# Two banded-mixing layers on one core: new instruction tables for both layers, three kinds of work moved between engines, and a setup in another order

## The chip, the cores and the metric

The kernel runs on one core of a Trainium2 chip. Its time is the device time of one launch in microseconds (us), of which the median over several runs counts; lower is better. The profile shows one execution. Its engines are called PE (TensorE, with PEld for its weight loads), DVE (VectorE), ACT (ScalarE), POOL (GpSimd) and SP (SyncE, which here only issues transfers). A name with q behind it (SPq, ACTq) is the engine's queue that issues transfers.

## The reference

The input `x` is a 512 x 512 image with 64 channels in float32. Two layers of the same form follow each other; each adds to `x` what it computes from a group norm of `x` over the whole image:

```python
def _gn(v, G=32, eps=1e-5):
    B_, H_, W_, C_ = v.shape
    g = v.reshape(B_, H_, W_, G, C_ // G)
    m = jnp.mean(g, axis=(1, 2, 4), keepdims=True)
    s = jnp.var(g, axis=(1, 2, 4), keepdims=True)
    return ((g - m) / jnp.sqrt(s + eps)).reshape(v.shape)
...
xn = _ln(x, norm_scale, norm_bias)
left = (xn @ Wl + bl) * mask * jax.nn.sigmoid(xn @ Wlg + blg)
right = (xn @ Wr + br) * mask * jax.nn.sigmoid(xn @ Wrg + brg)
out_gate = jax.nn.sigmoid(xn @ Wog + bog)
out = _banded_ingoing(left, right, WIN)
out = _ln(out, out_norm_scale, out_norm_bias) * out_gate
return out @ Wo + bo
```

There are 128 hidden channels. `_banded_ingoing` multiplies, per hidden channel, a band matrix of half width 4 (taken from `left` near the diagonal of the image) with `right`, so that each output row mixes the 9 nearest rows. The second layer cannot begin before the first has seen the whole image, since its group norm needs the sums over all of it.

## The kernel before

**Tiling.** The image's rows are cut into 9 blocks of 64 rows that overlap (`row_blocks`, line 145). In a block the columns are taken in two halves side by side on the 128 partitions and go through in 32 units of 8 columns, 8 units to a chunk, so a layer has 36 chunks and 288 units. A unit on its input side is loaded (`load`, line 474, two transfers into one of 12 z buffers), multiplied by the group norm's factor `ga` (`scaled`, line 515) and shifted by `gb` (`moved`, line 518), reduced to its layer norm's statistics (`inner_stats`, line 521), centred and rescaled, turned by TensorE (`transposed`, line 532), copied from PSUM twice (`kept`, `kept_again`), multiplied with the weights (`right`, line 587), gated, and written into the tile `RO`. On its output side, 16 units later, it passes the band product (`mix`, line 668), the second norm (`norm`, line 771), its gate, two more products, and is added to the image that `fetch` (line 819) has read anew and `stored` (line 852) writes.

**The bands.** Five extra units with negative numbers carry the pixels near the diagonal (`lefts`, `load_near`, line 485). They are loaded into the tile `A`, pass the same scaling, and give the band values `L9`, which `spread_left` writes to a table in HBM (`left_of`). From there `take_left` (line 654) reads one slab of the band matrices for the current block into `A`, four transfers of 128 KB a slab and eight slabs a block. The table is first filled with zeros from the tile `nothing`.

**The order.** All instructions of the layers go through `en` (line 458), which keeps them in program order on their engine. That order is written out by hand in two tables of 320 words, `FIRST` and `SECOND` (lines 38 and 71), one for each layer. `layer` (line 868) runs through its table once for each period, a period being one chunk of eight units. A word such as `norm6:0!@2` names a step, its part, how many units it lies behind the period's first (so `load:11` loads unit 11 while unit 0 is the period's own), with `!` for the step's other engine, and the PSUM buffer behind `@`. For `norm` the mark means POOL in place of ACT, for `copy` (the band product's way out of PSUM) DVE in place of ACT. `on_load` (line 909) also takes one waiting slab, ahead of the unit's own load. `on_copy` puts a slab in the list once the last chunk of a block has used it. Every transfer of the layers is issued by SP.

**The setup.** `fetch_layer` (line 264) issues some 70 small loads of weights and masks on ACT's queue. `input_stats` (line 397) streams the whole image through three buffers `gn_x`, 16 transfers of 4 MB on SP, and takes `bn_stats` on DVE; between the tiles `solve_layer` (line 297) folds the weights. Then the sums are closed on DVE and TensorE, `ga` and `gb` come out (`group_affine`, line 390), and the first layer begins. Between the layers `mid_stats` (line 1074) does the same from sums that the first layer has collected.

Of the kernel before, what the change touches and what calls it, by code (L numbers as in the profile page):

```python
# [43 lines left out]
last:0 fetch:1 end:0 turn0:1@1 move:11 copy:7 turn1:1@1 proj0:0@0 right1:0 tg:1 norm3:2 sig0:0
resc:2 resc:1 norm4:2 band:0@2 ost1:4 norm1:2 copy:0 right0:0 norm5:2! gate:2@1 ztr:1@0 scale:8
gated:2 norm6:2! sums:-2 last:1 keep0:1 keep1:1 fetch:2 ost0:7 ost2:5 norm2:2! stp:0 inner:6
norm7:2! band:1@2 sums:0 ztr:2@0 copy:1 ost0:5 keep0:2 turn1:2@1 ost1:6 inner:11 norm0:2! load:12
turn0:2@0 inner:5 proj0:1@2 move:8 keep1:2 sa:4 inner:8 norm0:3 scale:12 centre:9 tg:2 sig0:1
band:4@0 sd0:4 norm1:3 end:1 norm3:3! band:6@1 load:13 norm6:3 norm2:3! norm7:3! right0:1 sd1:4
resc:3 copy:4 sd2:4 gate:3@2 stp:-3 norm5:3! copy:6 gated:3 fetch:3 norm4:3! proj0:2@0 turn1:3@1  # L50
centre:4 turn0:3@2 band:5@2 tg:3 sig0:2 centre:6 norm2:4 right0:2 last:2 ztr:3@1 copy:5 end:2
gate:4@2 ost2:9 keep0:3 proj1:1@0 norm6:4! ost2:11 norm5:4! norm0:4 gated:4 load:14 norm7:4
norm3:4! ost2:12 norm1:4! sig1:1 last:3 scale:13 norm4:4 scale:14 sums:-1 ost2:15 ost1:13
turn1:4@2 centre:5 keep1:3 ost3:8 ost3:11 turn0:4@2 gate:5@1 resc:4 gated:5 ost2:10 ost0:11 resc:6
ost1:11 right1:1 tg:4 proj1:2@0 norm5:5! norm7:5! norm4:5! proj0:3@2 ost2:8 ost1:10 norm6:5
ztr:4@1 norm2:5! sig1:2 sig0:3 norm1:5! end:3 centre:8 keep0:4 right1:2 resc:5 right0:3 sums:3
fetch:4 norm3:5 norm0:5 keep1:4 last:4 centre:7 ost3:12 turn1:5@2 load:15 ost0:10 turn0:5@1 end:4
norm6:6 norm7:6! norm1:6 proj1:3@0 centre:10 tg:5 sig1:3 proj0:4@1 sig0:4 stp:-1 proj1:4@2 ost3:10
right1:3 norm4:6! ost1:8 ztr:5@0 norm5:6! sig1:4 fetch:5 right0:4 norm0:6 sums:1 ost0:8 keep0:5
ost3:9 last:5 sums:2 right1:4 load:16 gate:6@1 resc:7 keep1:5 ost1:9 ost0:9 gate:7@2 ost3:14 sa:8  # L60
ost3:13 turn0:6@0 norm2:6! norm3:6! gated:6 gated:7 norm0:7 ost0:14 sd0:8 scale:15 stp:1 fetch:7
move:15 turn1:6@0 sd1:8 norm4:7! norm1:7! centre:11 tg:6 fetch:6 end:5 proj1:5@1 proj0:5@2 sig1:5
ztr:6@0 norm7:7! norm5:7! norm6:7 load:17 sig0:5 norm2:7 right1:5 sums:4 keep0:6 last:6 norm3:7!
move:13 right0:5 ztr:7@2 keep1:6 keep0:7 keep1:7 turn0:7@0 turn1:7@1 sd2:8 proj0:6@1 proj1:6@2
tg:7 stp:3 stp:2 end:6 scale:17 norm5:8! resc:8 load:18 norm4:8 sig0:6 stp:4 fetch:8 sig1:6
# [3 lines left out]
seed:0 inner:8 turn1:1@2 inner:5 ztr:1@0 right1:0 move:11 ost3:5 stp:-1 keep0:1 turn0:1@2 norm5:2!  # L69
last:0 keep1:1 norm0:2 tg:1 inner:10 norm2:2 resc:2 centre:4 norm6:2! proj0:1@1 sa:4 sig0:1  # L70
proj1:1@0 norm7:2 end:0 sig1:1 right0:1 band:4@2 copy:4 ztr:2@1 right1:1 band:5@0 centre:5
centre:6 keep0:2 keep1:2 stp:0 sd0:4 norm3:2 seed:1 gate:2@2 inner:11 copy:5! fetch:2 norm4:2
norm1:2! gated:2 centre:3 proj0:2@1 turn0:2@0 turn1:2@2 band:7@2 norm0:3! norm7:3 sd1:4 last:1
resc:3 norm2:3! sig0:2 tg:2 norm3:3! gate:3@0 norm6:3 sd2:4 copy:7 norm4:3! norm5:3 norm1:3
gated:3 turn1:3@2 turn0:3@1 end:1 resc:4 move:9 right0:2 load:13 norm6:4 norm2:4 stp:1 tg:3
norm1:4! seed:2 band:3@1 norm3:4 norm0:4! copy:3 resc:7 inner:9 proj1:2@0 norm4:4 ost3:8 ztr:3@2
ost2:9 last:2 ost0:13 ost1:9 fetch:3 end:2 ost3:9 stp:2 keep0:3 sig1:2 right1:2 keep1:3 gate:4@1
resc:6 proj0:3@2 norm7:4! load:15 seed:3 ost1:15 norm5:4 ztr:4@0 gated:4 centre:10 ost0:9
turn0:4@1 centre:9 sig0:3 ost1:13 load:16 ost0:15 turn1:4@0 right0:3 last:3 keep0:4 keep1:4
norm4:5 tg:4 norm3:5 centre:8 norm1:5! norm6:5 norm7:5! resc:5 load:12 proj0:4@2 ost0:14 sig0:4  # L80
load:14 end:3 norm5:5 right0:4 proj1:3@1 ost3:10 norm0:5! sig1:3 right1:3 gate:5@0 gated:5
proj1:4@2 ztr:5@1 seed:4 ost1:11 turn0:5@0 norm2:5! sig1:4 ost0:11 turn1:5@2 ost3:14 last:4
scale:13 ost0:10 right1:4 keep0:5 scale:16 ost3:11 ztr:6@2 scale:12 norm4:6 tg:5 norm1:6! end:4
ost1:10 keep1:5 scale:14 keep0:6 proj0:5@1 move:12 keep1:6 proj1:5@0 ost2:11 norm5:6! fetch:6
sig0:5 seed:5 stp:3 ztr:7@2 right0:5 fetch:5 last:5 norm7:6 ost2:8 ost2:10 norm2:6! sig1:5
gate:6@1 right1:5 keep0:7 norm6:6! norm0:6 ost2:13 ost0:8 keep1:7 turn0:6@0 scale:15 norm3:6
turn1:6@2 proj1:6@2 fetch:9 gated:6 ost2:12 norm0:7! ost1:8 load:19 sa:8 sig1:6 norm5:7! end:5
norm7:7 tg:6 seed:6 norm4:7! norm3:7! proj0:6@1 right1:6 norm1:7 proj1:7@0 move:16 sd0:8 sig0:6
proj0:7@2 right0:6 norm2:7! sig1:7 gate:7@1 norm6:7! right1:7 sig0:7 right0:7 scale:19 gated:7
last:6 band:8@1 sd1:8 turn1:7@2 fetch:7 move:15 turn0:7@1 gate:8@0 sd2:8 load:17 copy:8 band:9@1  # L90
norm0:8 norm7:8 move:14 norm5:8 norm4:8 tg:7 norm1:8! move:13 load:18 norm6:8! norm2:8 end:6
ost1:12 seed:7 resc:8 turn0:8@2 copy:9 last:7 ztr:8@1 gated:8 norm3:8! resc:9 turn1:8@0 norm0:9!
inner:14 stp:5 ost3:12 norm1:9! inner:12 keep0:8 scale:18 band:14@0 keep1:8 ost2:14 norm5:9 stp:6
tg:8 proj0:8@1 stp:4 ost3:15 norm6:9! norm4:9! ost0:12 band:10@2 norm3:9! fetch:8 fetch:12 norm7:9
inner:15 copy:14 gate:9@0 scale:17 sig0:8 move:18 end:7 norm2:9 copy:10 right0:8 ost2:15 gated:9
proj1:8@1 centre:15 ost1:14 sig1:8
# [1123 lines left out]
```

## Time and profile before

| | us |
|---|---|
| median of the three runs | 4443.09 |
| the three runs | 4437.63, 7979.66, 4443.09 |
| the profiled execution | 4426.74 |
| its span, first to last instruction | 4425.0 |
| mean granted TensorE clock | 0.964 |

The span falls into five parts, cut at the first and the last `gated` step of each layer (an instruction ACT `ZH<-banks`, one a unit). A period is the time between the `gated` steps of unit 8n and unit 8n + 8.

| part | from, to (us) | length |
|---|---|---|
| statistics and weights, up to `gb` | 0 to 239.53 | 239.5 |
| filling of the first layer | 239.53 to 388.93 | 149.4 |
| first layer | 388.93 to 2359.66 | 1970.7 |
| between the layers, and filling of the second | 2359.66 to 2533.83 | 174.2 |
| second layer | 2533.83 to 4414.82 | 1881.0 |

The first `gated` steps of periods in the first layer stand at 388.93, 440.20, 492.89, 555.42 and 613.35, in the second at 2533.83, 2585.15, 2635.47, 2697.17 and 2747.44. Lines of the profile name almost every instruction of the layers as L456, the helper that records them; tiles tell them apart.

### The profile page before, as it was taken

How to read it: one execution, taken by the hardware profiler on the slowest of the kernel's cores; microseconds unless marked ns; L12 is line 12 of the kernel's file. 1: busy time of each engine (PE TensorE's matmuls, PEld its weight loads, DVE VectorE, ACT ScalarE, POOL GpSimd, SP SyncE). 2: the span in 40 equal slices, each digit the busy share in tenths (PEclk: the TensorE clock that was granted, in tenths of full speed). 3: DMA queues.
4: the chain of work that ended last, by engine and by line, in shares of the span. 5: the costliest groups of instructions: out<-in, count | busy, mean ns of one | idle time of the engine just before them, and what ended most of it. 6: DMA issues, size and time to landing. Idle time of an engine off the chain costs nothing. (4 is left out here: it accounts for less than half of the span.)

```text
span 4425.0 us, 223146 instructions
## 1 busy us (share of the span) xinstructions
PE 3777.6 (85%) x94986; PEld 3257.9 (74%) x94986; DVE 3645.9 (82%) x9884; ACT 3189.7 (72%) x5974; POOL 3713.9 (84%) x4839
## 2 busy tenths in 40 slices
PE   0138999999999999999994699989898998999998
PEld 0027888888888888888873687878787787878786
DVE  6967888888888888888875698989898888989897
ACT  0017777777777777777772587878787887878886
POOL 0059999999999999999954798989899898989893
PEclk9999999999999999999997799999999999999999
DMA  7843444444544444545442344444444444454533
GB/s 301 331 130 102 131 119 130 125 126 125 130 125 130 122 130 121 131 127 131 131 115 62 107 127 136 126 134 132 132 131 135 135 130 137 124 143 125 150 112 98
DMA packets 696443, 596.26 MB, mean 135 GB/s; under 512 B 139658, under 2 KB 552856, under 8 KB 692632
## 3 DMA queue, kind: packets, MB, share of 16 engines
q1 hardware_dynamic: 690272, 580.43, 45.3%
q8 instruction: 748, 12.26, 1.2%
q14 instruction: 247, 2.02, 0.2%
q10 hardware_dynamic: 5176, 1.55, 0.1%
HBM read 436.71 MB, written 149.74 MB: 133 GB/s over the span
## 5 line engine op out<-in xcount | busy, mean ns | idle before, releaser
L456 POOL TENSOR_SCALAR on<-RO,rs,nm 128x128 f32<-128x128 f32 x2520 | 1134.4, 469 | 161.1 <-PE banks L456 111.9
L456 ACT ACTIVATE on<-RO,nm,rs 128x128 f32<-128x128 f32 x2088 | 971.5, 499 | 116.7 <-PE banks L456 105.7
L456 PE MATMUL banks<-pack,ZT 64*128 64x128 f32 x9216 | 984.9, 286 | 30.0 <-DVE RO L456 12.5
L456 PE MATMUL banks<-pack,zT 64*128 64x128 f32 x9216 | 945.4, 278 | 0.3 <-issue 0.2
L456 ACT ACTIVATE sg<-banks 128x512 f32<-128x512 f32 x1170 | 696.7, 596 | 301.6 <-PE banks L456 280.8
L456 POOL TENSOR_TENSOR z<-z,ga 128x512 f32<-128x512 f32 x564 | 726.1, 1297 | 219.5 <-DMA z<-in_x_dram 105.0
L456 DVE TENSOR_TENSOR RO<-banks,sg 128x512 f32<-128x512 f32 x1152 | 777.2, 682 | 135.0 <-ACT sg L456 96.7
L456 PEld LDWEIGHTS banks<-pack,ZT 64*128 64x128 f32 x9216 | 774.9, 193 | 153.2 <-DVE RO L456 45.7
L456 DVE BATCH_NORM_STATS2 sto<-RO 128x6 f32<-128x256 f32 x2304 | 847.0, 413 | 3.9 <-ACT RO L456 2.6
L456 DVE SCALAR_TENSOR_TENSOR ZH<-banks,pack,ZH 128x896 f32<-128x896 f32 (+1 forms) x576 | 668.0, 1160 | 180.8 <-PE banks L456 150.3
L456 PEld LDWEIGHTS banks<-pack,zT 64*128 64x128 f32 x9216 | 755.6, 193 | 1.2 <-issue 0.6
L456 PE MATMUL banks<-RO,A 64*64 64x64 f32 x36864 | 694.0, 223 | 48.8 <-DVE RO L456 19.5
L456 PEld LDWEIGHTS banks<-RO,A 64*64 64x64 f32 x36864 | 617.8, 136 | 155.7 <-DVE RO L456 55.5
L456 POOL TENSOR_TENSOR z<-z,gb 128x512 f32<-128x512 f32 x564 | 724.1, 1291 | 3.1
L456 ACT COPY RO<-banks 128x1024 f32<-128x1024 f32 x540 | 539.5, 1008 | 196.4 <-PE banks L456 186.6
L456 PE MATMUL bank<-pack,ZH 128*64 128x64 f32 x18432 | 667.3, 226 | 11.3 <-DVE XR L456 7.2
L456 PEld LDWEIGHTS bank<-pack,ZH 128*64 128x64 f32 x18432 | 594.6, 139 | 71.2 <-issue 32.4
L456 ACT ACTIVATE ZH<-banks 128x896 f32<-128x896 f32 (+1 forms) x576 | 531.8, 930 | 140.2 <-PE banks L456 133.2
L456 DVE BATCH_NORM_STATS2 sti<-z 128x6 f32<-128x128 f32 x2304 | 498.1, 282 | 146.1 <-POOL z L456 138.7
L456 POOL TENSOR_TENSOR z<-z,rs 128x512 f32<-128x512 f32 x576 | 605.1, 1062 | 14.5 <-DVE rs L456 14.4
L456 POOL TENSOR_TENSOR z<-z,sti 128x512 f32<-128x512 f32 x576 | 611.0, 1076 | 1.6 <-DVE sti L456 1.4
L456 PE MATMUL banks<-ZT,pack 64*128 64x448 f32 (+1 forms) x2304 | 584.3, 583 | 12.9 <-DVE RO L456 8.7
(177 smaller groups left out, 4129.1 us busy)
## 6 DMA issues: line engine op xcount, KB each, us to landing
z<-in_x_dram SPq DMA_DIRECT2D x576, 128.0 KB
A<-left_of SPq DMA_DIRECT2D x576, 128.0 KB
z<-mid_x SPq DMA_DIRECT2D x576, 128.0 KB
gn_x<-in_x_dram SPq DMA_DIRECT2D x16, 4096.0 KB
XR<-in_x_dram SPq DMA_DIRECT2D x448, 112.0 KB
mid_x<-XR SPq DMA_DIRECT2D x448, 112.0 KB
XR<-mid_x SPq DMA_DIRECT2D x448, 112.0 KB
out_dram<-XR SPq DMA_DIRECT2D x448, 112.0 KB
```

Of the source, the lines that this page charges most:

```text
L456: return lambda *a, **k: tc.keep_in_program_order(f(*a, **k))
```

## The change

**Tables.** Both tables are written anew; they hold the same 320 steps a period in another order. The engines that they choose differ so: in `FIRST` 33 of the 64 norms are on POOL in place of 38, and one of eight copies, one of eight scale steps and one of eight move steps are on DVE; in `SECOND` 35 norms are on POOL in place of 32, one copy is on DVE as before, and two scale and two move steps are on DVE. A scale or move step was on DVE only for even units up to number 11 and for three of the extra units; now it is for those that the table marks and for even units up to number 23 (`which`). The places of the loads, by their order in the table and in parts of a period ahead of the unit's scale step: `FIRST` had 0.47, 0.07, 0.07, 0.04, 0.03, 0.14, 0.03 and 0.16, and has 0.09, 0.05, 0.11, 0.31, 0.65, 0.26, 0.29 and 0.24; `SECOND` had 0.14, 0.17, 0.07, 0.08, 0.10, 0.27, 0.11 and 0.30, and has 0.18, 0.24, 0.06, 0.04, 0.73, 0.18, 0.24 and 0.07.

**Extra units.** They now live in five of the twelve z buffers, so seven units are loaded early in place of twelve. In the first layer their loads are issued ahead of everything else of the layer, before the sums are closed; in the second after the first half of the generator, ahead of the load of `left_w`. They are turned at the table's `ztr` step, no longer at `proj`.

**Setup.** The weight loads are issued on POOL's queue in place of ACT's. The sums of the group norm are gathered while the tiles stream, on POOL for all but the last tile. The folding of the weights, the rest of the stores, the early loads and the zeros of `left_of` come ahead of the closing of the sums. `nothing` is a small constant tile, and the clearing of `XR` and `ZH` is put into the first periods of layer one.

```diff
 FIRST = """
...
-right0:-2 norm6:0! right1:-2 proj0:-1@0 norm0:0! proj1:-1@1 sig0:-1 ztr:0@2 move:9 norm1:0 ost1:7
...
+norm2:0 resc:0 norm3:0! scale:8 norm1:0! norm6:0! move:8! norm4:0! norm0:0 proj0:-1@0 norm7:0
...
-        load = nc.scalar.dma_start
+        load = nc.gpsimd.dma_start
...
+            def gather(t: int, engine):
+                if t == 0:
+                    engine.tensor_copy(own, parts[:, :, 0:2, 2])
+                    return
+                off = two(f"gn_off{t % 2}")
+                engine.tensor_tensor(off, parts[:, :, 2 * t : 2 * t + 2, 1], ref, sub)
+                engine.tensor_tensor(s1, s1, off, add)
+                engine.tensor_tensor(off, off, off, mult)
+                engine.tensor_tensor(s2, s2, off, add)
+                engine.tensor_tensor(own, own, parts[:, :, 2 * t : 2 * t + 2, 2], add)
...
                 for g in range(G):
                     en.vector.bn_stats(st[:, g, t, :], xt[:, :, 2 * g : 2 * g + 2])
+                gather(t, en.gpsimd if t < n_t - 1 else en.vector)
                 meanwhile(t)
-            parts = st.rearrange("p g t (s k) -> p g (t s) k", k=3)
-            nm = 2 * n_t
...
-            nc.vector.tensor_reduce(mean, parts[:, :, :, 1], AX.X, ALU.add)
-            nc.vector.tensor_scalar(mean, mean, 1.0 / nm, None, ALU.mult)
-            nc.vector.tensor_tensor(off, parts[:, :, :, 1], last(mean, nm), ALU.subtract)
-            nc.vector.tensor_reduce(own, parts[:, :, :, 2], AX.X, ALU.add)
-            nc.vector.tensor_tensor(off, off, off, ALU.mult)
-            nc.vector.tensor_reduce(between, off, AX.X, ALU.add)
...
+            afterwards()
+
+            mean, var = two("gn_mean"), two("gn_var")
+            nc.vector.scalar_tensor_tensor(mean, s1, 1.0 / n_t, ref, mult, add)
...
+            nc.vector.tensor_tensor(var, s1, s1, mult)
+            nc.vector.scalar_tensor_tensor(var, var, -1.0 / n_t, s2, mult, add)
+            nc.vector.scalar_tensor_tensor(var, own, 1.0 / nt, var, mult, add)
...
     def load(src: bass.AP, u: Unit):
+        u.z = zp.tile([P, JU, D], F32, tag=f"z{u.at % NZ}", name="z")
         if u.near is not None:
-            two = A[:, u.near // (2 * JU)].rearrange("p h i t -> p (h i t)")
-            u.z = two.rearrange("p (n j c) -> p n j c", n=2, c=D)[:, u.near // JU % 2]
             load_near(src, u)
             return
...
+        if stats:
+            for n in range(2):
+                posts.setdefault(n - 1, []).append(lambda n=n: clear_zh(ZH[n]))
+            for n in range(NX):
+                posts.setdefault(n, []).append(lambda n=n: clear_xr(XR[n]))
...
-        EARLY = NZ
-        for t in range(EARLY):
+        early = [t for t in range(NZ) if t - NZ not in lefts]
+        if stats:
+            for t in sorted(lefts):
+                load(src, lefts[t])
+        for t in early:
             load(src, units[t])
         yield
+        if not stats:
+            for t in sorted(lefts):
+                load(src, lefts[t])
         unused = onp.tile([P, JQ, H], F32, tag="on0", name="on")
         w["left"] = unused[:, :2].rearrange("p j h -> p (j h)")
         en.sync.dma_start(w["left"], left_w[0 if stats else 1])
-        which = lambda u: en.vector if u.at < NU + 4 and u.at % 2 == 0 else en.gpsimd
+        which = lambda u, alt: en.vector if alt or (u.at < 3 * NU and u.at % 2 == 0) else en.gpsimd
...
         def on_scale(n, t, alt, b):
             for u in inputs(t):
-                scaled(u, which(u))
+                scaled(u, which(u, alt))
...
+        def afterwards():
+            for _ in solving:
+                pass
+            next(one)
+            for z in left_of.rearrange("a (p m w) -> a p m w", p=P, w=WIDE):
+                en.sync.dma_start(z, mid(nothing, z.shape[1]))
+
+        input_stats(meanwhile, afterwards)
```

More of the change, by code (lines that the diff above doesn't have):

```diff
@@ L44 @@
[L44 to L65, printed above, removed]
+norm2:0 resc:0 norm3:0! scale:8 norm1:0! norm6:0! move:8! norm4:0! norm0:0 proj0:-1@0 norm7:0
+sig1:-1 ost0:5 right1:-1 sig0:-1 ztr:0@1 last:-1 right0:-1 keep0:0 sums:-3 keep1:0 move:7
@@ new lines @@
+stp:-2 copy:7 move:10 turn1:2@1 ost3:5 proj1:0@0 copy:5 turn0:2@0 load:12 ost1:4 inner:9 inner:10
+tg:2 norm3:3 centre:4 resc:3 sig1:0 sa:4 band:6@2 copy:6 norm2:3! resc:2 centre:5 last:1 sums:-4
+norm7:3! right1:0 ztr:2@1 proj0:1@0 centre:9 norm5:3 norm1:3 keep0:2 norm6:3! sd0:4 load:14
+keep1:2 norm4:3! sig0:1 norm0:3 band:4@2 gate:3@1 sd1:4 copy:4 right0:1 centre:8 sd2:4 ost1:11
+end:1 turn0:3@0 turn1:3@0 scale:11 proj1:1@2 resc:4 fetch:4 gated:3 ztr:3@1 tg:3 norm0:4! norm7:4
+norm5:4 sig1:1 right1:1 sums:-1 keep0:3 norm3:4 norm1:4 fetch:2 keep1:3 ost2:11 ost0:11 last:2
@@ new lines @@
+proj1:4@2 ost2:13 norm1:6 gate:6@0 norm6:6 norm7:6! norm3:6 gated:6 ost3:9 proj0:4@1 sig1:4
+inner:11 ost0:14 norm2:6! norm5:6 fetch:5 sums:3 norm0:6! scale:15 last:5 ost1:9 sig0:4 right1:4
+ztr:6@2 scale:13 right0:4 sa:8 turn0:6@0 sd0:8 turn1:6@2 tg:6 proj1:5@1 keep0:6 keep1:6 gate:7@2
+sd1:8 norm7:7! sig1:5 end:5 norm3:7 centre:11 proj0:5@0 sums:1 norm0:7! norm2:7! stp:2 last:6
+sig0:5 gated:7 right1:5 right0:5 norm5:7 sd2:8 resc:7 ztr:7@0 keep0:7 load:16 move:13 norm1:7!
+keep1:7 gate:8@1 proj0:6@2 gated:8 proj1:6@0 ost3:14 resc:9 fetch:6 end:6 norm4:7 sig0:6 norm6:7!
@@ L66 @@
+scale:12! sig1:6 turn1:7@1 turn0:7@0 right0:6 sums:6 move:14 proj1:7@2 right1:6 norm5:8 tg:7
 """
 SECOND = """
[L69 to L96, printed above, removed]
+centre:7 inner:6 norm0:2 gate:2@1 keep1:2 sig1:1 seed:1 fetch:1 move:11 ost0:6 band:4@2 last:1
@@ L97 @@
+turn1:9@1 norm6:10! centre:16 norm3:10 load:19 fetch:8 turn0:9@2 norm4:10 norm5:10 fetch:11
+right1:8 ztr:10@2 load:21 copy:13! keep0:10 tg:9 norm1:10 scale:19 norm2:10 ost3:13 last:8 end:8
+centre:12 proj1:9@0 ost1:13 norm7:10!
 """
@@ L190, in tile_two_banded_layers @@
     left_rows = dram.tile([P, H // 2 * NEAR * JQ * 2], F32, name="left_rows")
+    nothing = const.tile([P, WIDE], F32, name="nothing")
+    nc.gpsimd.memset(nothing, 0.0)
     ident = const.tile([P, P], F32, name="ident")
@@ L911, in on_load @@
                 take_left(*slabs.pop(0))
-            for u in inputs(t):
-                if t not in units or t >= EARLY:
-                    load(src, u)
+            if t in units and t not in early:
+                load(src, units[t])
         def on_scale(n, t, alt, b):
             for u in inputs(t):
-                scaled(u, which(u))
+                scaled(u, which(u, alt))
         def on_move(n, t, alt, b):
             for u in inputs(t):
-                moved(u, which(u))
+                moved(u, which(u, alt))
         def on_inner(n, t, alt, b):
```

143 lines of the change are left out of this document (88 added, 55 removed).

## The prediction

> **What bounds the kernel now.** I read four views in this order: the busy times by stretch, cut at the stages and then at single periods; the waits of a stretch; the issuing queue SP in order of time; and the groups of instructions of two normal periods. The stages first (columns: busy us and instructions of PE, PEld, DVE, ACT, POOL, then granted clock, DMA share, GB/s):
>
> ```profile
> 0.74:239.53 238.79, 23.97 (x48) 12.19 (x48) 195.57 (x622) 1.28 (x1) 2.58 (x5) 1.00 0.79 316
> 239.53:388.93 149.40, 74.27 (x1256) 64.20 (x1256) 92.50 (x302) 56.47 (x102) 107.91 (x94) 0.91 0.35 97
> 388.93:2359.66 1970.73, 1832.45 (x48222) 1597.16 (x48224) 1614.20 (x4301) 1517.54 (x2793) 1793.13 (x2426) 0.98 0.47 125
> 2359.66:2533.83 174.17, 86.08 (x1544) 74.35 (x1538) 100.65 (x327) 58.38 (x106) 106.84 (x96) 0.74 0.32 88
> 2533.83:4414.82 1880.99, 1756.70 (x43843) 1506.50 (x43843) 1640.42 (x4331) 1555.01 (x2975) 1702.40 (x2215) 0.97 0.45 129
> ```
>
> Four periods make a block. One block of each layer, cut at the periods' `gated` steps:
>
> ```profile
> 837.12:888.81 51.69, 50.86 (x1363) 44.69 (x1352) 45.15 (x121) 43.09 (x81) 51.61 (x71) 1.00 0.44 117
> 888.81:941.50 52.69, 51.46 (x1376) 45.00 (x1376) 46.14 (x125) 43.29 (x81) 52.61 (x71) 1.00 0.45 117
> 941.50:1006.30 64.80, 54.87 (x1404) 47.27 (x1408) 48.26 (x131) 43.71 (x81) 54.99 (x74) 0.95 0.53 143
> 1006.30:1061.40 55.10, 52.11 (x1363) 45.83 (x1352) 44.64 (x119) 43.07 (x81) 50.71 (x68) 0.97 0.45 125
> ...
> 2747.44:2797.76 50.32, 49.28 (x1264) 42.55 (x1262) 46.76 (x126) 44.40 (x86) 50.08 (x65) 1.00 0.43 121
> 2797.76:2848.10 50.34, 49.30 (x1264) 42.51 (x1262) 46.82 (x126) 44.38 (x86) 50.06 (x65) 1.00 0.43 118
> 2848.10:2912.02 63.92, 52.55 (x1264) 45.20 (x1262) 47.34 (x127) 44.48 (x86) 50.12 (x65) 0.89 0.57 162
> 2912.02:2962.62 50.60, 49.10 (x1262) 42.63 (x1260) 46.80 (x126) 44.32 (x86) 50.03 (x65) 1.00 0.38 118
> ```
>
> In a normal period POOL is busy 99.4 to 99.8% of the time and PE 98%: both bound it, POOL first. In the third period of a block the same 1264 PE instructions take 63.92 us. Against four normal periods (52.19, the mean of the first two rows, and 50.33) a block of layer one carries 224.28 - 208.8 = 15.5 us too much, one of layer two 215.18 - 201.3 = 13.9. That period is the one in which the next block's slabs come in:
>
> ```profile
> POOL z L456 <- DMA z<-mid_x: 10.1, 3, 5.5
> DVE XR L456 <- DMA XR<-mid_x: 9.2, 1, 9.2
> ...
> 2880.06 2.58 SPq L456 DMA_DIRECT2D A<-left_of  x4
> 2882.75 1.19 SPq L456 DMA_DIRECT2D z<-mid_x  x2
> 2883.98 3.32 SPq L456 DMA_DIRECT2D A<-left_of  x4
> 2887.34 1.26 SPq L456 DMA_DIRECT2D z<-mid_x  x2
> ```
>
> These are the waits from 2848 to 2912 and SP's queue in it. SP issues without a pause; each slab puts 2.6 to 3.3 us ahead of the unit loaded with it, and of the `XR` behind. So POOL waits 10.1 us for z and DVE 9.2 for `XR`: a transfer issued late, not a slow engine. The granted clock falls to 0.89, and PE's busy time rises by 3.3 of the 13.6 us.
>
> **The change, part by part.**
>
> **Setup.** SP's waits in the first 62 us, DVE's in the first 75, then DVE in order of time:
>
> ```profile
> SPq L456 <- DMA raw<-in_L_conv_Wrg_dram: 21.9, 1, 21.9
> SPq L456 <- DMA brow<-in_L_conv_blg_dram: 19.3, 1, 19.3
> SPq L456 <- DMA ci<-in_L_conv_src_mask_dram: 18.8, 1, 18.8
> ...
> DVE gn_st L456 <- DMA gn_x<-in_x_dram: 38.3, 4, 11.7
> ...
> 14.21 10.54 DVE L456 BATCH_NORM_STATS2 gn_st<-gn_x 128x6 f32<-128x256 f32 x32 [10.24 <-DMA gn_x<-in_x_dram]
> 227.00 1.50 DVE L418 TENSOR_REDUCE gn_mean<-gn_st 128x32 f32<-128x1024 f32 x1
> 239.31 0.22 DVE L395 SCALAR_TENSOR_TENSOR gb<-gn_mc,ga 128x64 f32<-128x64 f32 x1
> 256.53 0.69 DVE L456 TENSOR_TENSOR A<-A,ga 128x512 f32<-128x512 f32 x1 [9.42 <-DMA A<-in_x_dram]
> ```
>
> SP held tiles two to four back, though their buffers were free, for weight loads on ACT's queue. With these on POOL's queue I take that wait as gone: of DVE's 38.3 us only the first 10.2 stay, -28. That cover goes if POOL issues slowly: DVE needs the 19th load (`brow`) after three tiles, at 14.2 + 3 x 10.5 = 46 us, 2.3 us a load. No row prices a POOL issue; the gain lies between 0 (SP held as before) and 28, and I take 28, as the rows name only ACT's loads. The closing sums take 12.3 us (227.00 to 239.31). Five wide operations of up to 1.5 us leave, about eight of 0.22 come: -5 (0 to -7). The extra units' loads no longer wait for `gb` and freed memory: 256.53 - 239.53 = 17 us go; behind them comes POOL's own work. -17 (0 to -25, since the later loads trickled in too). They stand on SP behind the last tile, with seven units' loads: 22.7 us for such a train of 13 (row below) and 14 x 0.6. The last tile is issued three tiles of 10.5 us before its own work, so the 31 us just fit; what does not fit delays the first scaling. The `XR` clears move into DVE's idle time in the filling (92.5 busy of 149.4). POOL's gathers run beside the stream, with 2.58 us of POOL work so far. Setup: -50.
>
> **Between the layers.** SP, and POOL's first use:
>
> ```profile
> 2368.74 0.40 SPq L1183 DMA_DIRECT2D pack<-spare  x1
> 2376.05 0.34 SPq L456 DMA_DIRECT2D on<-left_w  x1
> 2376.56 22.73 SPq L456 DMA_DIRECT2D A<-mid_x  x13
> ...
> 2381.70 1.26 POOL L456 TENSOR_TENSOR A<-A,ga 128x512 f32<-128x512 f32 x1 [19.51 <-DMA A<-mid_x]
> ```
>
> The 13 loads go ahead of `left_w`, which waits for the sums: 2376.56 - 2369.1 = 7 us earlier, -7 (0 to -10). Five of twelve early loads now wait for the extra units; I cost that at nothing, because these loads have the 22.73 us train ahead of them anyhow, and keep +5.
>
> **Normal periods.** The prices, from two periods of layer two, and of scale and move on DVE over the whole span:
>
> ```profile
> L456 POOL TENSOR_SCALAR on<-RO,rs,nm 128x128 f32<-128x128 f32 x64 | 29.4, 480 | 0.3 <-DVE nm L456 0.3
> L456 POOL TENSOR_TENSOR z<-z,gb 128x512 f32<-128x512 f32 x17 | 22.0, 1303 | 0.0
> L456 POOL TENSOR_TENSOR z<-z,ga 128x512 f32<-128x512 f32 x16 | 20.6, 1308 | 0.2 <-DMA z<-mid_x 0.2
> L456 DVE COPY RO<-banks 128x1024 f32<-128x1024 f32 x2 | 2.5, 1225 | 0.0
> ...
> L456 DVE TENSOR_TENSOR z<-z,ga 128x512 f32<-128x512 f32 x12 | 13.0, 1100 | 0.0
> L456 DVE TENSOR_TENSOR z<-z,gb 128x512 f32<-128x512 f32 x12 | 12.9, 1080 | 0.0
> ```
>
> Layer one: POOL loses 5 x 0.48 and 2 x 1.3, 52.6 - 5.0 = 47.6. DVE gains a copy and two z steps, 46.1 + 1.2 + 2.2 = 49.5. PE keeps its 51.5 of 52.69 and becomes the bound, with 1.2 us of gaps. I let 0.5 of them go: -18 over 36 periods (bounds: -1.2, PE without a gap, and +0.5, should DVE's longer queue hold PE back).
>
> Layer two: POOL loses 4 x 1.3 and gains 3 x 0.48, 50.06 - 3.8 = 46.3. DVE gains 4 x 1.09: 46.82 + 4.4 = 51.2, above today's 50.33. DVE without a gap makes that the period, +0.9, +32 over 36. The best end is PE at 49.3 (-1.0, -36), if the z steps cost the shortest row, 0.69 us; the worst, with the longest, stands under the rivals (+78).
>
> The z steps on DVE are dear because of POOL: alone 0.69 us, on average 1.09. [...]
>
> **Slab periods.** The number of slab transfers stays, 32 a block at 2.58 / 4 = 0.65 us, 21 us of SP. What changes is where they stand. In `SECOND` the loads that draw the first four slabs stood within 0.24 to 0.43 of a period; now three stand in 0.22 to 0.46, two at its end, three in the next. In `FIRST` five of eight loads now lead their scale step by 0.24 to 0.65 of a period (12 to 34 us), where six had 0.03 to 0.16. A slab's 3 us fits into such a lead. What is late next are the units that still lead by 0.04 to 0.11 (2 to 6 us), two or three in each table, and `XR`. So I take 9 of 15.5 us away in layer one and 8 of 13.9 in layer two, over 8 block changes each: -72 and -64. Bounds: nothing, and all (-124, -111).
>
> Part of that is the clock, 0.89 granted in that period. [...]
>
> **Sum**, against the profiled execution (4426.74): -50 - 7 - 18 - 72 + 32 - 64 = -179, so 4247.7. The median of the runs, 4443.09, lies 16.35 above that execution; I put the change's median as far above its own: 4264 us.
>
> **The rivals.**
>
> *The slab periods stay.* The transfers only move to other late units. For it: their number and SP's order within a load are as before, and SP is the same queue. Against: the leads above. Then -50 - 7 - 18 + 32 = -43: 4400 us.
>
> *DVE bounds layer two harder.* Where POOL worked beside it, DVE's z steps took longer:
>
> ```profile
> 2430.87 4.25 DVE L456 TENSOR_TENSOR z<-z,ga 128x512 f32<-128x512 f32 x3
> ```
>
> At 4.25 / 3 = 1.42 us DVE has 46.82 + 5.7 = 52.5, +2.2 x 36 = +78 in place of +32: 4310. Against it: norms of 0.48 us on POOL end sooner than its z steps of 1.3.
>
> *Every period becomes like the slab period (slower).* Short leads of 0.04 to 0.09 stand in both new tables, and each late z makes POOL wait. At the 10.1 us of the slab period, in all 72, it is 72 x 10.1 = 727 us, less the 15.5 and 13.9 that each block already has (235) and the 57 of setup and turn: 4443 + 435 = 4878. From 4.1 us a period on nothing is gained, from 5.3 on it is slower by over 2%. Against: leads of 0.03 and 0.04 stood in the old table, and normal periods show 0.2 us of such waits in two periods.
>
> *The setup is not freed,* as POOL's issue is as slow as ACT's was: 28 us less gain, 4292.
>
> **How the numbers follow.** Forecast 0.58, with 4185 to 4350 as its own range; slab periods stay 0.16; DVE harder 0.12; slower 0.08; setup not freed 0.06. The predicted time is that of the likeliest. The low end takes layer two at PE's floor and a few us more off the slabs (4264 - 68 - 11); the high end, 4410, takes in the rival at 4400. A measurement of this kernel tells about 2%, 89 us, from no change, so under 4354 counts as faster: the forecast nearly whole, the setup case, and half of the DVE case, which has slab waits of its own: 0.70. Within 2% 0.22, slower 0.08.
>
> **What would show it.** Tiles two to four of `gn_x` issued in the first microseconds, no SP wait for weights; `gb` near 207 us, the first scaling right behind it. In layer one normal periods of 51 to 52 us with PE, not POOL, at 98%; in layer two DVE above 98%. Slab periods under 60 us with the clock above 0.89. Wrong would be: z waits of POOL in normal periods, slab periods at 64, a layer two period above 52.5, or DVE idle in it while the period has not moved.

## The result and the profile after

The changed kernel takes 4497.59 us (median of four runs, 4483.48 to 4508.68), against 4437.63 for the kernel before (median of 4430.08, 4437.63 and 4443.09; its run of 7979.66 us, slow for a reason that isn't known, is left out): a ratio of 1.0135 [1.009, 1.018]. It is slower by 1.35%, where a gain of 4% was forecast. The profiled execution has a span of 4481.7 us, 56.7 above before.

The busy times of the same five parts (columns as before: length, then PE, PEld, DVE, ACT, POOL, granted clock, DMA share, GB/s):

```profile
0.74:213.53 212.79, 24.05 (x48) 12.17 (x48) 191.29 (x626) 1.28 (x1) 65.76 (x155) 1.00 0.87 339
213.53:333.02 119.49, 65.03 (x1192) 56.29 (x1194) 100.72 (x302) 53.47 (x93) 87.27 (x73) 0.93 0.50 141
333.02:2338.28 2005.26, 1831.69 (x48285) 1603.80 (x48284) 1759.49 (x4417) 1557.29 (x2949) 1675.62 (x2189) 0.98 0.46 123
2338.28:2496.02 157.74, 80.47 (x1378) 69.66 (x1378) 105.49 (x323) 52.88 (x96) 87.92 (x75) 0.73 0.37 100
2496.02:4472.27 1976.25, 1781.86 (x44011) 1518.19 (x44011) 1855.65 (x4483) 1534.13 (x2875) 1612.86 (x2196) 0.96 0.43 123
```

Everything up to the first `gated` step is 55.9 us shorter (388.93 to 333.02), the turn between the layers 16.4 (174.17 to 157.74). Layer one is 34.5 us longer and layer two 95.3. In the two layers DVE has gained 145.3 and 215.2 us of busy time, 4.0 and 6.0 us a period, where the sum had 3.4 (two z steps and a copy) and 4.4 (four z steps). In a normal period of layer two it is 7.4 us (54.20 against 46.82).

One block of each layer, cut at the periods:

```profile
781.67:835.76 54.09, 50.89 (x1381) 45.03 (x1380) 50.53 (x129) 44.33 (x86) 49.09 (x64) 1.00 0.42 113
835.76:889.92 54.16, 50.95 (x1381) 44.91 (x1380) 50.50 (x129) 44.18 (x86) 49.05 (x64) 1.00 0.44 113
889.92:950.78 60.86, 52.74 (x1381) 46.46 (x1380) 50.58 (x128) 44.28 (x86) 49.04 (x64) 0.97 0.55 146
...
2771.49:2826.44 54.95, 50.55 (x1260) 43.28 (x1261) 54.20 (x131) 43.90 (x83) 46.96 (x64) 0.97 0.41 111
2826.44:2886.70 60.26, 52.60 (x1259) 45.18 (x1260) 54.47 (x130) 43.76 (x82) 47.11 (x64) 0.92 0.56 155
```

The slab periods (third and fifth row) have come down from 64.80 and 63.92 to 60.86 and 60.26, with the clock at 0.97 and 0.92: close to the sign that was named. This block isn't typical of layer one: over its eight full blocks the third period takes 63.1 us on average, where before it took 61.1; in layer two it went from 62.7 to 59.5. The normal periods have gone up: 54.1 in layer one (PE 94% busy, no engine full) and 54.95 in layer two, where DVE is busy 98.6% of the time.

What DVE does with it, in 110 us (about two periods) of layer two (columns: busy us, mean ns of one, idle before), and then in order of time, first DVE and then POOL:

```profile
L477 DVE TENSOR_TENSOR z<-z,ga 128x512 f32<-128x512 f32 x4 | 9.7, 2424 | 0.0
L477 DVE TENSOR_TENSOR z<-z,gb 128x512 f32<-128x512 f32 x4 | 6.8, 1704 | 0.0
```

```profile
2773.70 4.01 DVE L477 TENSOR_TENSOR z<-z,ga 128x512 f32<-128x512 f32 x1
2777.64 0.68 DVE L477 TENSOR_TENSOR RO<-banks,sg 128x512 f32<-128x512 f32 x1
...
2779.17 2.74 DVE L477 TENSOR_TENSOR z<-z,gb 128x512 f32<-128x512 f32 x1
...
2782.16 0.67 DVE L477 TENSOR_TENSOR z<-z,gb 128x512 f32<-128x512 f32 x1
...
2773.43 1.27 POOL L477 TENSOR_TENSOR z<-z,gb 128x512 f32<-128x512 f32 x1
2774.66 1.28 POOL L477 TENSOR_TENSOR z<-z,ga 128x512 f32<-128x512 f32 x1
2775.89 1.27 POOL L477 TENSOR_TENSOR z<-z,gb 128x512 f32<-128x512 f32 x1
2777.13 1.34 POOL L477 TENSOR_SCALAR on<-RO,rs,nm 128x128 f32<-128x128 f32 x2
...
2779.31 1.05 POOL L477 TENSOR_TENSOR z<-z,sti 128x512 f32<-128x512 f32 x1
2780.32 1.04 POOL L477 TENSOR_TENSOR z<-z,rs 128x512 f32<-128x512 f32 x1
2782.78 1.48 POOL L477 TENSOR_SCALAR on<-RO,rs,nm 128x128 f32<-128x128 f32 x3 [1.42 <-PE banks L477]
```

A z step on DVE takes 2.06 us on average ((9.7 + 6.8) / 8), not 1.09. The one at 2782.16 runs while POOL waits, and takes 0.67. The one at 2773.70 is on record as running for 4.01 us, but it ends 0.6 us after POOL has gone from its z steps to norms: it stood through three POOL instructions, and everything behind it on DVE stood with it. Of the 116 such steps between 2700 and 4350 us, 65 took less than 0.9 us (0.68 on average), one 1.44, 28 from 2.1 to 2.8 (2.71 on average) and 22 from 4.0 to 4.4 (4.31). The 22 ended beside a norm of POOL. In 26 of the 28, as in the one at 2779.17, POOL had run out of work before the step ended.

### The profile page after: what moved, and what is told of

The parts are those of the page before. It is cut to its first block, busy times and chain, and to the rows that moved or that the text cites. A ratio compares the mean times of both kernels' runs of the same rounds, so it can differ in the third digit from the quotient of the medians.

```text
span 4481.7 us, 222948 instructions
## 1 busy us (share of the span) xinstructions
PE 3786.4 (84%) x94986; PEld 3262.7 (73%) x94986; DVE 4015.5 (90%) x10148; ACT 3200.8 (71%) x6012; POOL 3530.1 (79%) x4689
## 4 chain that ended last, share of the span: by engine, by line
PE 52%; DVE 23%; DMA 7%; issue 7%; POOL 4%; SPq 4%; ACT 2%; DVEq 0%; POOLq 0%; ACTq 0%
PE banks L477 40%; PE bank L477 10%; SPq L477 4%; DVE RO L477 4%; DVE ZH L477 4%; DVE sti L477 3%; DVE sto L477 3%; POOL z L477 3%; DVE XR L477 2%; PE acc L477 2%; DVE z L477 2%; DVE gn_st L477 2%; POOL on L477 1%; DMA XR<-in_x_dram 1%; ACT sg L477 1%
## 5 line engine op out<-in xcount | busy, mean ns | idle before, releaser
L477 PEld LDWEIGHTS banks<-pack,ZT 64*128 64x128 f32 x9216 | 762.4, 191 | 236.6 <-DVE RO L477 75.9
L477 PE MATMUL banks<-pack,zT 64*128 64x128 f32 x9216 | 932.3, 275 | 0.8 <-issue 0.8
L477 DVE BATCH_NORM_STATS2 sto<-RO 128x6 f32<-128x256 f32 x2304 | 868.2, 413 | 2.3 <-ACT RO L477 2.3
L477 DVE TENSOR_TENSOR RO<-banks,sg 128x512 f32<-128x512 f32 x1152 | 761.2, 679 | 63.0 <-ACT sg L477 57.1
L477 PEld LDWEIGHTS banks<-RO,A 64*64 64x64 f32 x36864 | 647.2, 143 | 227.2 <-issue 117.4
L477 PE MATMUL banks<-RO,A 64*64 64x64 f32 x36864 | 716.1, 229 | 74.5 <-issue 58.9
L477 POOL TENSOR_TENSOR z<-z,sti 128x512 f32<-128x512 f32 x586 | 624.7, 1067 | 37.5 <-DVE sti L477 37.5
L477 POOL TENSOR_TENSOR z<-z,ga 128x512 f32<-128x512 f32 x457 | 585.9, 1285 | 81.8 <-DMA z<-mid_x 41.1
L477 ACT COPY RO<-banks 128x1024 f32<-128x1024 f32 x504 | 505.7, 1011 | 187.8 <-PE banks L477 180.8
L477 POOL TENSOR_TENSOR z<-z,gb 128x512 f32<-128x512 f32 x454 | 583.0, 1290 | 25.1 <-DVE z L477 23.8
```

The costliest lines, as they stand in the source:

```text
L477: return lambda *a, **k: tc.keep_in_program_order(f(*a, **k))
```

## The experiments

To compare them, each layer is cut into normal periods (mean of the first and second period of the eight full blocks), what a block takes beyond four of these (mean over the eight; the slabs come in there), and the last, shorter block. All from the `gated` steps of the profiled execution, in us. A ratio is against the kernel before as it ran beside that kernel (medians from 4432.0 to 4437.6):

| kernel | median | ratio | first gate | layer 1: normal, extra, last | turn | layer 2: normal, extra, last |
|---|---|---|---|---|---|---|
| before | 4437.63 | | 388.9 | 52.49, 13.9, 179.5 | 174.2 | 50.73, 11.5, 165.2 |
| changed | 4497.59 | 1.0135 [1.009, 1.018] | 333.0 | 54.36, 9.6, 189.1 | 157.7 | 54.78, 5.8, 177.1 |
| z_on_pool | 4460.83 | 1.0063 [1.0039, 1.0087] | 336.0 | 54.49, 8.3, 188.9 | 153.7 | 54.36, 4.1, 175.9 |
| psum_l2 | 4387.05 | 0.9893 [0.9871, 0.9915] | 335.3 | 54.38, 10.3, 189.9 | 151.9 | 50.91, 9.7, 170.6 |
| psum_both | 4319.20 | 0.9741 [0.972, 0.9761] | 328.4 | 52.99, 9.0, 187.5 | 150.0 | 50.80, 9.8, 173.3 |
| old_tables | 4376.65 | 0.9876 [0.9852, 0.99] | 344.3 | 52.63, 13.2, 178.9 | 165.3 | 50.76, 11.7, 165.2 |
| loads_on_act | 4510.60 | 1.0173 [1.0148, 1.0199] | 359.1 | 54.60, 8.5, 190.6 | 156.9 | 54.80, 5.8, 176.7 |
| two_slabs | 4374.07 | 0.987 [0.9845, 0.9896] | 331.9 | 52.87, 13.8, 185.6 | 150.4 | 50.95, 11.3, 171.2 |
| no_slabs | 4175.20 | 0.9423 [0.9395, 0.9452] | 328.6 | 53.08, -0.4, 187.7 | 151.5 | 50.87, -0.2, 174.9 |
| slab_behind | 4305.37 | 0.9726 [0.9706, 0.9745] | 328.1 | 53.10, 8.3, 187.3 | 154.6 | 51.08, 6.5, 170.9 |

**The marked z steps back on POOL** (`z_on_pool`), the tables otherwise as changed:

```diff
-        which = lambda u, alt: en.vector if alt or (u.at < 3 * NU and u.at % 2 == 0) else en.gpsimd
+        which = lambda u, alt: en.vector if u.at < 3 * NU and u.at % 2 == 0 else en.gpsimd
```

> The changed kernel, with the marked scale and move steps (one of each a period in layer one, two of each in layer two) on POOL again; both new tables otherwise as they are. [...] Then layer two loses 8.3 us of DVE work a period and gains 4 x 1.29 on POOL: POOL 46.95 + 5.2 = 52.1 bounds it, period near 52.2, DVE near 46 busy; layer one near 52.2. Total about 4482 - 36 x 2.7 - 36 x 1.9 = 4316 us in the profiled execution. Theory B: the order of the new tables itself is worse (dependent steps too close, TensorE waits). Then the periods stay at 54 and 55 us and the total at 4480.

```profile
2932.51:2986.64 54.13, 49.05 (x1259) 42.08 (x1260) 46.78 (x126) 43.42 (x82) 51.18 (x68) 1.00 0.39 113
```

```profile
PEld banks L477 <- POOL on L477: 9.8, 9, 2.0
DVE sti L477 <- POOL z L477: 9.1, 2, 4.6
```

These are a normal period of layer two, and two rows of the waits of two such periods. DVE has fallen to 46.78 us, and the period has hardly moved: POOL, 51.18 busy, is now late in an order that was written for a POOL without these steps, and PE's weight loads and DVE wait for it. Taken alone, this is the outcome of theory B, the order, and not of z steps that stand on DVE. But undoing the move doesn't tell what the move cost, since the places in the tables stay. So the cost had to be taken out with the steps left where they are.

**The factors in PSUM** (`psum_l2` in layer two, `psum_both` in both). `ga` and `gb` are copied once into a free part of a PSUM bank, and DVE's z steps read them there. Order, engines and arithmetic stay:

```diff
+    by = [(ga, gb), (ga, gb)]
+    def to_psum(bank: bass.AP):
+        by[1] = bank[:, :D], bank[:, D : 2 * D]
+        for to, of in zip(by[1], by[0]):
+            nc.vector.tensor_copy(to, of)
...
-        engine.tensor_tensor(u.z, u.z, mid(ga, JU), ALU.mult)
+        engine.tensor_tensor(u.z, u.z, mid(by[engine is en.vector][0], JU), ALU.mult)
...
+    to_psum(acc_bank[:, P + 8 * NB :])
...
+    to_psum(work[0][:, 8 * NB :])
```

> The changed kernel, with a copy of ga and gb in a free part of the PSUM bank that holds the roots, read in layer two by DVE's scale and move steps (POOL reads SBUF as before); same order, same engines. Theory A (port): a z step on DVE has one SBUF input left and takes 0.7 us in place of 2.06 on average, longest under 1 us; DVE's busy time in a normal period of layer two falls from 54.2 by 5.5 to 48.7, PE becomes the bound, period 50.0 to 50.6 us; layer two 36 x 4.4 = 158 us shorter, total about 4324. Theory C: the long DVE steps are waits for a transfer or for another engine that the profile counts as busy time. Then they stay at 2.7 and 4.3 us and the period at 54.9. Theory B (table order): steps short, but the period still 54 or more.

> As the kernel before this one, and in layer one too: the copy stands in the bank in which TensorE sums the second layer's statistics. Theory A: layer one's DVE z steps fall from 3.1 and 0.8 us to 0.7 each, DVE from 50.5 to about 48, normal period 54.1 to about 52, layer one 70 us shorter, total about 4250. If the shared bank makes DVE and TensorE wait for each other, layer one stays at 54 or grows; then the total is that of the kernel with layer two alone, or more.

The z steps of two periods of layer two, then a normal and the slab period of each layer, in `psum_both`:

```profile
L477 DVE TENSOR_TENSOR z<-z,work 128x512 f32<-128x512 f32 x8 | 5.4, 672 | 0.0
```

```profile
823.16:875.18 52.02, 51.08 (x1381) 45.13 (x1380) 47.97 (x129) 44.07 (x86) 47.99 (x64) 1.00 0.46 118
875.18:936.14 60.96, 52.74 (x1381) 46.45 (x1380) 48.12 (x128) 44.27 (x85) 47.97 (x64) 0.97 0.57 148
...
2858.51:2908.79 50.28, 48.78 (x1258) 42.00 (x1260) 48.67 (x130) 43.55 (x82) 46.41 (x64) 1.00 0.43 121
2960.24:3015.85 55.61, 50.66 (x1260) 43.42 (x1260) 48.99 (x130) 43.61 (x83) 46.37 (x64) 0.97 0.61 165
```

The eight steps take 0.67 us on average, beside a POOL as busy as in the changed kernel (46.41 us of a normal period, 46.96 there). In `psum_l2` layer two falls by 98.7 us (1976.2 to 1877.5). That is less than theory A's 158: the normal period falls by 3.9 us, but a block's extra rises from 5.8 to 9.7. Layer one, where only `psum_both` reads PSUM, falls by 57.5 there (2012.4 to 1954.9), against the 70 expected. From the changed kernel to `psum_both` the two layers lose 149 us: so much did the wait of DVE's z steps cost the change, more than the whole loss. `psum_both` is faster than both kernels.

**The tables of before** in the changed kernel (`old_tables`; the diff is the two strings):

> The changed kernel with both tables of before: the new setup, the extra units in z buffers and the early DVE share are what is left of the change. If the setup's gain (first gated step at 333.0 in place of 388.9) and the turn between the layers (157.7 in place of 174.2) are independent of the tables: 4425 - 56 - 16 = 4353 us span, periods 52.2 and 50.3, slab periods as before (64 us). If the turn's gain belongs to the tables: 4369. If the new load scheme disturbs the old tables, longer than 4400.

The setup's new order and the turn are worth -44.6 and -8.9 us without the tables; 11 and 8 us more come with the tables, which also order the filling. The span of 4371.5 us is near the case in which the turn's gain belongs to the tables (4369), but by another sum: half of the turn's gain stays, and 11 us of the setup's go. With the old tables a block's extra is back at 13.2 and 11.7 us: the gain at the slabs belongs to the tables.

**The weight loads back on ACT's queue** (`loads_on_act`; `load` and the small saves at the end of the setup):

```diff
-        load = nc.gpsimd.dma_start
+        load = nc.scalar.dma_start
...
-                nc.gpsimd.dma_start(pieces[n : n + 1], piece[:1])
+                nc.scalar.dma_start(pieces[n : n + 1], piece[:1])
```

> The changed kernel with the weight loads and the setup's small saves issued on ACT's queue again, all else as changed. Theory A (these loads held SP back, as the prediction had it): SP waits some 60 us for raw, brow and ci again, DVE's wait for gn_x goes from 12 back to about 38 us, gb from 213.4 to about 240, the first gated step from 333 to about 360, the median about 4525. Rival B (the gain came from the order of the closing sums and the extra units' loads): gb within 5 us of 213, the median within 0.2% of 4497. Rival C (a part only, because gathers and saves moved too): gb between 220 and 235. Layers and turn are as in the changed kernel in all three.

SP's waits in the first 62 us and DVE's in the first 335, with these loads on ACT, and then the same two views of the changed kernel:

```profile
SPq L477 <- DMA raw<-in_L_conv_Wrg_dram: 22.3, 1, 22.3
SPq L477 <- DMA brow<-in_L_conv_blg_dram: 19.2, 1, 19.2
```

```profile
DVE gn_st L477 <- DMA gn_x<-in_x_dram: 39.8, 4, 11.7
```

```profile
SPq L477 <- DVE gn_st L477: 31.1, 3, 10.5
SPq L477 <- DMA gn_x<-in_x_dram: 13.1, 2, 12.2
```

```profile
DVE gn_st L477 <- DMA gn_x<-in_x_dram: 12.3, 2, 11.1
...
DVE brow L477 <- issue: 4.2, 1, 4.2
```

The waits for `raw` and `brow` come and go with the queue, DVE's wait for the image goes from 12.3 to 39.8 us (a third wait of SP, 18.7 us for `ci`, follows within the first 75 us). `gb` comes 22.6 us later (236.14 against 213.54) and the first `gated` step 26.0. The medians differ by 13 us, less than their intervals tell apart; the profiled executions by 25.4. In the changed kernel SP waits for DVE to free a buffer and for the image itself, no longer for weights.

**The slabs.** `two_slabs` takes up to two ahead of one load, `no_slabs` none after the first block (so that the later blocks compute other values), `slab_behind` takes the slab behind the load; all three start from `psum_both`:

```diff
-            if slabs:
+            for _ in slabs[:2]:
                 take_left(*slabs.pop(0))
```

```diff
         held[h] = n
+        if n:
+            return
```

```diff
-            if slabs:
-                take_left(*slabs.pop(0))
             if t in units and t not in early:
                 load(src, units[t])
+            if slabs:
+                take_left(*slabs.pop(0))
```

> The fastest kernel so far (ga and gb for DVE's z steps in PSUM in both layers, 4319 us) with up to two waiting slabs taken ahead of one unit's load instead of one. There a block's four periods carry about 10 us more than four normal ones in both layers. Theory A (what a slab delays on SP is the unit behind it, and the new tables have leads for one slab of 2.6 to 3.3 us but not for two): the extra goes up towards the 15.5 and 13.9 us of the kernel before, 3 to 5 us a block, 16 blocks, 4370 to 4400. Rival B (the extra is the sum of the slabs' time on SP and the DMA engines, however they are grouped): 4319 within 0.3%.

> The same fastest kernel, in which the slabs of blocks two to nine aren't read: these blocks compute with the band matrices of the first block, so the output differs there. Theory A (the slab transfers and the delays they cause are the whole extra of a block): the third and fourth period come down to the others, 52.6 and 50.6 us, some 160 us less, about 4160. Rival B (part of the extra is other work at the end of a block, the writes of the next block's bands and the clock): a half of it stays, about 4240. Rival C (the slabs are hidden by now): above 4290.

> The fastest kernel so far (4319 us) with each slab taken behind its unit's load on SP instead of ahead of it. Theory A (a block's extra of some 9.5 us is mostly the unit that stands behind a slab on SP): the extra falls by 3 us or more a block, 16 blocks, 4270 or less. Rival B (the next transfers on SP, the image rows for XR and the unit after, come late instead): 4319 within 0.5%. Rival C (the slab itself is what is late, so that taking it later costs): above 4340.

The third period of the same block of layer two, in the three kernels in this order:

```profile
3002.32:3064.89 62.57, 53.57 (x1260) 46.03 (x1261) 49.60 (x130) 43.43 (x83) 46.31 (x64) 0.92 0.59 162
```

```profile
2872.91:2923.89 50.98, 48.81 (x1260) 42.01 (x1262) 48.69 (x130) 43.63 (x83) 46.33 (x64) 1.00 0.38 117
```

```profile
2958.12:3014.57 56.45, 50.62 (x1260) 42.87 (x1261) 49.19 (x130) 43.46 (x83) 46.27 (x64) 0.97 0.59 164
```

Without the slabs a block carries nothing extra, and the clock is 1.00 in all eight periods of one block of each layer: the slabs and what they delay are all of it, 144 us of the time (4319.20 to 4175.20). Two at once bring back the extra of the kernel before in layer one (13.8) and nearly in layer two (11.3 of 11.5, though from 9.8 this is only 1.5 of the 3 to 5 us expected), and cost 51 us by the spans and 55 by the medians: it does matter how many stand ahead of one unit. Behind the unit's load, a block of layer two is 2.2 us shorter (4 x 51.08 + 6.5 against 4 x 50.80 + 9.8), one of layer one 0.2: that the next transfers pay for the rest, as rival B has it, fits but isn't shown. The median is 14 us lower, within 0.5% and not beyond the intervals, and the lowest of those that read all slabs.

**DVE's wait by itself.** `port` and `port_late` add short sequences behind the last period of the changed kernel (one execution each, with every sequence three times):

```python
def probe(kinds, late):
    en.gpsimd.tensor_tensor(d, d, mid(gb, JU), ALU.mult)   # frees DVE's step on d
    pool_run(kinds)                                        # T: 128x512 product, N: norm 128x128
    for k in range(late):                                  # only in port_late
        dd = d[:, 2 * k : 2 * k + 2, :].rearrange("p j c -> p (j c)")
        en.vector.tensor_tensor(spot, dd, spot, ALU.mult)
    en.vector.tensor_tensor(d, d, mid(ga, JU), ALU.mult)
```

> The changed kernel, with short sequences added behind its last period that take no part in the output: one POOL instruction on a tile frees a DVE instruction on the same tile while POOL goes on with a run of further instructions on other tiles, without a gap. Runs of 0, 1, 2, 3, 4, 6 and 8 products of 128x512 (1.28 us each), of 1, 4 and 8 norms of 128x128 (0.48 us), and mixed ones; the DVE instruction reads two tiles in SBUF, or one in SBUF and one in PSUM, or is a tensor_scalar or bn_stats with one input. Theory A (the DVE step with two SBUF inputs stands until POOL's run ends): its duration grows with the run, about 0.67 + 1.2 k us for k products, near 10 us for eight; with PSUM or one input it stays below 1 us. Theory B (it waits only for the instruction that POOL is at, as the prediction had it): at most 1.9 us from k = 1 on, the same for 2 and for 8. Theory C (a limit of some instructions, or POOL yields on a change of operation): it grows up to a few products and then stays, or a norm between the products ends the wait. For runs of norms A gives 4.4 us at eight, B at most 1.1.

From `port` in order of time: four products; two products, a norm, two products; four products with DVE's factor in PSUM; four products with a tiny copy on DVE; and four products with a tensor_scalar, which has one input in SBUF. POOL's rows with x4 and x2 hold so many instructions in one go.

```profile
4515.86 5.37 POOL L477 TENSOR_TENSOR probe_z<-probe_z,ga 128x512 f32<-128x512 f32 x4
4515.93 1.73 DVE L477 TENSOR_TENSOR probe_z<-probe_z,ga 128x512 f32<-128x512 f32 x1 [4.81 <-POOL probe_z L477]
...
4547.12 2.48 POOL L477 TENSOR_TENSOR probe_z<-probe_z,ga 128x512 f32<-128x512 f32 x2
4547.19 3.00 DVE L477 TENSOR_TENSOR probe_z<-probe_z,ga 128x512 f32<-128x512 f32 x1 [4.42 <-POOL probe_z L477]
4549.59 0.93 POOL L477 TENSOR_SCALAR probe_on<-RO,ga,gb 128x128 f32<-128x128 f32 x1
...
4560.85 0.69 DVE L477 TENSOR_TENSOR probe_z<-probe_z,work 128x512 f32<-128x512 f32 x1 [4.90 <-POOL probe_z L477]
...
4566.88 4.92 POOL L477 TENSOR_TENSOR probe_z<-probe_z,ga 128x512 f32<-128x512 f32 x4
...
4567.68 4.15 DVE L477 COPY probe_z<-probe_st 128x6 f32<-128x6 f32 x1
...
4573.27 1.47 DVE L477 TENSOR_SCALAR probe_z<-probe_z 128x512 f32<-128x512 f32 x1 [1.44 <-POOL probe_z L477]
```

Theory A, that DVE's step stands until POOL's run ends, falls: with one to eight products the step takes 1.73 or 1.74 us each time, as theory B has it. It ends some 0.6 us after the first product (an estimate, with 4.92 / 4 = 1.23 us a product), and POOL takes longer too: 5.37 us for these four products, 4.92 for the four beside the copy. Beside norms alone the step takes 0.69 us (one or four norms) or 0.76 (eight), hardly more than the 0.67 at 2782.16 us of the changed kernel, where POOL was idle. But with a norm two places further on it took 3.00 us, through both products, and ended beside the norm. The tiny copy took 4.15 us, through what was left of four products, until POOL's run ended, and the tensor_scalar took 1.47: one input in SBUF isn't enough to stay below 1 us, where theory A had said so. The three repeats of each agree to 0.01 us.

> The changed kernel with further short sequences behind its last period that take no part in the output. In the sequences before, a DVE step that came 0.07 us after the start of a POOL instruction stood for one instruction, 1.73 us, whatever the run's length, while in the layers 49 steps stood for three or four, and these had come 0.27 to 0.36 us into an instruction. Here DVE first does 0 to 4 short instructions of one SBUF and one PSUM input, so that its step comes later into POOL's first instruction; the runs are six products on separate tiles, six on one tile (each needs the one before), and norm, three products, norm, three products, on separate tiles and on one. Theory A (the moment of arrival decides: who comes after POOL's next instruction was already lined up loses turn after turn): 1.73 us at no delay and 2.9 to 7 us at the later ones, alike for separate tiles and one. [...] Theory C (a norm in the run decides, since the only sequence of products that stood longer had one): only the sequences with norms stand longer, up to the norm.

```profile
4584.97 0.45 POOL L477 TENSOR_SCALAR probe_on<-RO,ga,gb 128x128 f32<-128x128 f32 x1
4585.01 0.29 DVE L477 TENSOR_TENSOR work<-probe_z,work 128x128 f32<-128x128 f32 x1 [9.26 <-POOL probe_z L477]
4585.34 4.31 DVE L477 TENSOR_TENSOR probe_z<-probe_z,ga 128x512 f32<-128x512 f32 x1
4585.39 3.70 POOL L477 TENSOR_TENSOR probe_z<-probe_z,ga 128x512 f32<-128x512 f32 x3
4589.07 0.91 POOL L477 TENSOR_SCALAR probe_on<-RO,ga,gb 128x128 f32<-128x128 f32 x1
```

And the same run of POOL, met without a short instruction ahead:

```profile
4575.01 0.98 POOL L477 TENSOR_SCALAR probe_on<-RO,ga,gb 128x128 f32<-128x128 f32 x1
4575.06 0.69 DVE L477 TENSOR_TENSOR probe_z<-probe_z,ga 128x512 f32<-128x512 f32 x1 [6.39 <-POOL probe_z L477]
```

The first rows are norm, three products, norm, with DVE's step 0.37 us into the first norm. It stands for 4.31 us, through all three products, and ends beside the second norm: the picture of the layers (4.33 to 4.35 for 18 of the 22, with a norm and three z steps). Later arrivals stand until the same norm (3.96, 3.63, 3.30). But at 0.05 us into the first norm the step doesn't stand at all: it takes 0.69, beside that norm. Beside products alone, on separate tiles or on one, the step takes at most 1.75 us at every delay (1.08 behind two short instructions, 0.75 behind three), so neither the moment of arrival (A) nor the dependence of the products on each other explains the long waits by itself, though among norms the moment does count. Chained products between norms leave gaps of 0.08 us on POOL, and there the step takes 0.69 to 2.18 us. Theory C holds in so far as the step stood for more than one instruction in sequences with norms only. That the wait lasts up to a norm does not hold for all: 26 of the layers' 28 steps of 2.1 to 2.8 us had norms in front and none behind, and ended after POOL ran out of work. In `port` (by the sequence before) and `port_late` norms stood in front as well as behind, so the runs don't tell which of the two matters. The copy in `port`, another kind of instruction, took 4.15 us beside its products without any norm. What ends the wait is open; that a DVE step stood for 2.1 to 4.35 us, two to four POOL instructions, beside mixed runs of norms and z steps without a gap is shown.

## Why the prediction was wrong

**The step that failed** is "Normal periods", with its price of a z step on DVE: 1.09 us, the mean of 24 steps (twelve of each kind). These stood in the fillings at the layers' starts, where POOL often waits (107.91 of 149.40 us busy, by the stage's row), and none took longer than 1.75. In the normal periods, POOL runs norms and z steps without a gap for stretches, and there the same instruction costs 2.06 us on average and up to 4.35. In layer two four steps take 8.2 us in place of 4.4, and the period is 54.78 in place of 51.2 (+4.1 a period on before, where +0.9 stood), above the 52.5 that the prediction had named as the sign of being wrong. The rival "DVE bounds layer two harder" named the right cause and the right row, but took 1.42 us as the worst. Its argument against itself, that norms end sooner than z steps, holds for norms alone (0.69 to 0.76 us in `port`) and was the wrong way round for what POOL does here: beside runs with norms among the z steps DVE's steps took up to 4.35 us.

That DVE's step waits only for the instruction that POOL is at (theory B of `port`) holds for products alone (1.73 or 1.74 us, with one to eight of them). For norms and products mixed it doesn't: there a step stood for several instructions (3.00 us in `port`, 4.31 in `port_late`). The steps that have their factor in PSUM took 0.67 us on average in the layers (`psum_both`) and 0.69 in `port`; the tensor_scalar and the copy of `port`, with one input in SBUF, took 1.47 and 4.15.

**Layer one** was forecast at 51.7 a period with PE as the bound; it came to 54.36 with no engine full. DVE had gaps there, and yet its standing steps (2.90 us for the scale step, 0.81 for the move step, on average over the layer) made 1.4 us of the period: with the factors in PSUM it is 52.99. That is still 0.5 above before, so PE did not lose its gaps even then; what sets this 0.5 was not tried.

**The slab periods** went the right way, at half the size in layer one and a fifth in layer two. I took the excess from one block (15.5 and 13.9); over eight blocks it is 13.9 and 11.5. With DVE freed it is 9.0 and 9.8, so the tables give 4.9 and 1.7 us a block, -39 and -14 us, where -72 and -64 stood. In the changed kernel itself layer two shows only 5.8: a period that DVE stretches to 55 us probably has room for some of the slabs' delay, so reading the gain there flatters it. The leads were the right thing to look at: two slabs ahead of one load undo the gain. (Seven loads of the old `FIRST`, not six, led by 0.03 to 0.16.) Nor does shortening the waits bring the clock back by itself: in the third period shown of layer two the longest waits for a transfer are 2.3 us and PE's longest idle stretch is 2.95, against 9.2 and 4.81 before, and the granted clock is still 0.92, against 0.89.

**A term that was missing**: each layer's last block, with its draining, takes 10 and 12 us longer with the new tables, and still 8 longer with PSUM (187.5 and 173.3 against 179.5 and 165.2).

**Setup and turn** went the right way: -55.9 where -50 stood, -16.4 where -7 stood, outside its bounds of 0 to -10. That the setup's sum came so near is in part luck. Up to `gb` it gained 26.0 us where 33 stood, 22.6 of them by the weight loads (28 forecast); the filling gained 29.9 where 17 stood, and 11 of the whole came with the tables, for which the sum had nothing here. In the turn -8.9 came without the new tables, close to the forecast, and the rest with them. `gb` came at 213.31, not near 207: DVE still waits 11.1 us for one tile, and before its step on `brow` it stands idle for 4.2 us without a wait that the profile shows (rows above). The first scaling stands right behind it, by DVE in order of time:

```profile
213.31 0.22 DVE L398 SCALAR_TENSOR_TENSOR gb<-gn_mc,ga 128x64 f32<-128x64 f32 x1
213.46 1.75 DVE L477 TENSOR_TENSOR z<-z,ga 128x512 f32<-128x512 f32 x1
```

Added up by the spans: setup -55.9, layer one +34.5, turn -16.4, layer two +95.3, tail -0.8: +56.7. Without DVE's wait (`psum_both`) the layers are at -15.8 and -3.5, where -90 and -32 were forecast: the wait explains some 149 of the 236 us by which the sum was off, the size of the slab gain and the last blocks most of the rest.
